# Layer 1's attention: every second tile squared by ACT straight out of PSUM, with reordered transposes, sends and sums in layer 0

## The chip, the cores and the metric

The kernel runs on one core of one Trainium2 chip. The metric is the device time of one execution in microseconds, as the median of several runs. PE is the matrix engine (TensorE), DVE the vector engine, ACT the scalar engine, POOL is GpSimd and SP issues transfers. L12 is line 12 of the kernel before.

## The reference

A decoder of two layers works on x, 32 sequences of 100 tokens with 256 values each. A layer is three residual steps, each on a layer norm of x:

```python
x = x + _L0_attn_ref(_layernorm(x), w_qkv, w_proj)              # causal, 16 heads of 16
x = x + _L0_xattn_ref(ctx_768, _layernorm(x), mask, ...)        # over 361 context rows
x = x + _L0_ffn_ref(_layernorm(x), ...)                         # attention, then 8 experts
x = x + _L1_attn_ref(_layernorm(x), ...)
x = x + _L1_xattn_ref(_layernorm(x), ctx_768, ...)
x = x + _L1_ffn_ref(_layernorm(x), ...)                         # 8 experts with hidden layer
```

`_L0_ffn_ref` contains a second causal attention of 16 heads (with rotary queries and keys), a layer norm, a gate that picks the best 2 of 8 experts for every token, and another layer norm:

```python
x1 = _layer_norm(x + attn_out, ln1_w, ln1_b)
_, top_idx = jax.lax.top_k(softmax(x1 @ gate_w.T + gate_b), 2)
moe_out = sum(gate * (x1 @ expert_w + expert_b) for the two)
return _layer_norm(x1 + moe_out, ln2_w, ln2_b)
```

Layer 1's attention sends every head's queries and keys through a small network and a rotation, and uses sums of squares:

```python
def prep(t):
    h1 = jnp.tanh(jnp.einsum('bshd,do->bsho', t, w1) + b1)
    return jnp.einsum('bsho,on->bshn', h1, w2) + b2
qq = jnp.sum(qe ** 2, -1); kk = jnp.sum(ke ** 2, -1)    # qe, ke: prep(Q), prep(K), rotated
attn = jax.nn.softmax(s / s, axis=2)                    # s = qq * kk
```

## The kernel before

The 32 sequences (B) stand in 8 groups (NG) of 4 (G); a group's tile has GT = 400 columns, four sequences of 100 tokens. The stages follow one another: layer 0's attention to about 285 us, its cross attention to 740, the attention in its ffn to 1040 with a last iteration to 1055, the blocks of the experts to 1176, layer 1's attention to 1528, its cross attention to 2700, and its ffn. Each engine runs its instructions in the order in which the program names them, except for POOL and SP, whose issues the helper `in_order` also keeps in that order. A wait of one instruction so holds everything behind it on its engine.

**`heads_attention`** serves layer 0's attention and the ffn's. One iteration handles one sequence s (`i = s % 4` is its place in the group) as a software pipeline. PE computes the scores of s + 1 (`scores`), DVE adds the mask (`masked`, L372), then takes the negated maximum of each row (L383), and POOL adds it (L384, both in `lowered`). ACT takes exponentials (`exponentials`, L389), in two halves of 8 heads. For s itself `turn_weights` transposes the exponentials on PE in four rows r of four heads each (L396; rows 0 and 1 read the first half, 2 and 3 the second), and ACT copies each row out of PSUM to eT (L401). `sums` multiplies them by the values (L412) and ACT copies the result to back (L417). For s - 1, `divided` transposes back (L425), DVE takes a reciprocal (L430) and multiplies (L432) to o; `turn_sums` transposes o (L438, copy L444) and `output` projects it (L230). All of these PSUM tiles come from one rotating set, `mm_tile`, so that a transpose can begin only when the tile's former content has been read. `fill(s, part)` is called at four places of an iteration and puts in work of other stages.

In the ffn, `fill` follows a table, `plan`, whose keys are the distance of groups and whose entries are (i, part). `res` adds the attention's output to xl (L1396), whose norm `ahead_norm` and `rows_of` turn (L776 transposes xl). `gating` picks experts and places, and **`send0(g, i, behind, which)`** writes the rows of sequence i of group g to their experts' places in memory, with one indirect DMA of POOL for each of the two choices k (L1517), each behind a small memset (L1513). Groups 0 to 4 fill the first list, 5 to 7 the second.

**The expert blocks** are 65 (ALL), of 128 rows of one expert; the first list has M = MOST[0] = 39 of them. Block n fetches its rows six or more blocks ahead, `turned0` transposes them (L1620) and DVE (even n, L1628) or ACT (odd n, L1626) evicts the transposes with 1 added, `product` multiplies by the expert's weights (L230), ACT copies y out (L1646) and issues its DMA. After each block a hand-written table, `todo`, calls further work: the remaining `gating`, and from M + 5 on the sums of groups 0 and 1 (`weighed`, L1296), their second norm (`second_norm`, `second_scaled` on ACT, L199, and `second_added`), and `project_group(0, 0..10)`, which prepares group 0 for layer 1's attention: its norm xn (L190), the transposes of xn (part 2, L1191), the queries and keys (qk, L1205), the mean rows xm (L1211), vm and own (L1231). `halves` places the sends of the last groups and the fetches of the sums (`outputs_back`, L1287), paced by a copy of one value of the next block's tile.

**Layer 1's attention** has 16 turns for each group. A turn calls `second` for the tile of four turns before, then `first`: eight score products (L1928) and two tanh on ACT (L1934). `second` adds products (L1947) into one PSUM tile in two calls; with the second (o = 1, turns 1, 3, 5, ...) DVE evicts the tile with bias b2h to y (L1960), and squares it (L1971) into one quarter of sq. The last group's last tile does both on ACT (L1958, L1969); groups 6 and 7 rotate y before they square it. A tile is named by m (0 to 3) and r2 (0, 1). `head_sums` adds a group's squares on PE and DVE copies the sums out (L2008). `around` places the next group's `project_group` parts and the last group's sums between the turns.

Of the kernel before, what the change touches and what calls it, by code (L numbers as in the profile page):

```python
# [14 lines left out]
AF = mybir.ActivationFunctionType  # L15
ALU = mybir.AluOpType
# [3 lines left out]
B, T, D = 32, 100, 256  # L20
S2, DC = 361, 192
G = 4
NG = B // G
GT = G * T
# [42 lines left out]
def kernel(ctx: ExitStack, tc: tile.TileContext, io: dict, out: bass.AP):  # L67
# [218 lines left out]
    def heads_attention(pool, w, wo, bias, norm, turn, res, fill, ready=0, order=()):  # L286
# [102 lines left out]
            nc.scalar.activation(ex, sms.pop((s, hf)), AF.Exp, scale=0.25)  # L389
            exs[s, hf] = ex  # L390

        def turn_weights(s):
            for r in range(4):
                pt = mm_tile()
                for j in range(4):
                    nc.tensor.transpose(  # L396
                        pt[:T, j * T : (j + 1) * T], exs[s, r // 2][:, 4 * (r % 2) + j, :],
                        ident[:T, :T],
                    )
                eT = pool.tile([T, 4, T], F32, tag="eT", name="eT", bufs=5)  # L400
                nc.scalar.copy(eT.rearrange("p j q -> p (j q)"), pt[:T, :GT])  # L401
                eTs[s, r] = eT
            exs.pop((s, 0)), exs.pop((s, 1))

        def sums(s):

# [48 lines left out]
        with in_order(*order):  # L455
            for part in range(4 if ready < 1 else 0):
                norm(0, part)
            turned_[0] = turn(0)
            for m in range(4):
                queries_or_keys(0, m)  # L460
            if ready == 2:
                norm(1, 3)
            values(0)
            ps = scores(0)
            for hf in range(2):
                masked(0, hf, ps[hf])
                lowered(0, hf)
                exponentials(0, hf)
            if ready == 2:
                turned_[1] = turn(1)  # L470
                for m in range(2):
                    queries_or_keys(1, m)
            for part in range(4 if ready < 2 else 0):
                norm(1, part)
            for s in range(B + 1):
                g, i = s // G + 1, s % G
                more = s + 1 < B
                if more:
                    ps = scores(s + 1)
                    masked(s + 1, 0, ps[0])  # L480
                if g < NG and (bias is None or g == 1):
                    if i == 0 and g not in turned_:
                        turned_[g] = turn(g)
                    for m in (((2,), (3,), (), ()) if ready == 2 else ((0,), (1,), (2, 3), ()))[i]:
                        queries_or_keys(g, m)
                if i >= 1 and bias is None and g + 1 < NG:
                    norm(g + 1, i - 1)
                fill(s, 0)
                if 1 <= s <= B:
                    divided(s - 1)  # L490
                if more:
                    lowered(s + 1, 0)
                    masked(s + 1, 1, ps[1])
                if s < B:
                    turn_weights(s)
                fill(s, 1)
                if more:
                    lowered(s + 1, 1)
                    values(s + 1)
                if 1 <= s <= B:  # L500
                    turn_sums(s - 1)
                if more:
                    exponentials(s + 1, 0)
                if s < B:
                    sums(s)
                fill(s, 2)
                if 1 <= s <= B:
                    output(s - 1)
                if more:
                    exponentials(s + 1, 1)  # L510
                if i == 3 and bias is None and g + 1 < NG:
                    norm(g + 1, 3)
                    turned_[g + 1] = turn(g + 1)
                fill(s, 3)
# [788 lines left out]
        )  # L1303

    def second_scaled(g, half_):
        scaled(x1back[g], x1back[g], range(2 * half_, 2 * half_ + 2), last_sums[g])

    def second_added(g, half_):
# [6 lines left out]
    with tc.tile_pool(name="f0x", bufs=1) as fixed, tc.tile_pool(name="f0", bufs=2) as pool:  # L1315
# [298 lines left out]
        def turned0(n):  # L1614
            if n >= ALL:
                return
            xg = xgs.pop(n)
            pt = mm_tile()
            for c in range(2):
                nc.tensor.transpose(  # L1620
                    pt[:, c * P : (c + 1) * P], xg[:, c * P : (c + 1) * P], ident
                )
            xT = tiles.tile([P, 2, P], F32, tag="xgT", name="xgT", bufs=4)
            flat = xT.rearrange("p c t -> p (c t)")
            if n % 2:
                nc.scalar.activation(flat, pt[:, : 2 * P], AF.Identity, bias=ones8[:, 0:1])  # L1626
            else:
                nc.vector.tensor_scalar_add(flat, pt[:, : 2 * P], 1.0)  # L1628
            xgTs[n] = xT
# [25 lines left out]
        def ahead_norm(g, part):  # L1655
# [15 lines left out]
            },  # L1671
            0: {(3, 2): ((rows_of, 0),)},
            -3: {
                (0, 2): ((send0, 0),), (1, 2): ((send0, 1),), (2, 2): ((send0, 2),),
                (3, 2): ((send0, 3),),
            },
            -1: {
                (1, 2): ((rows_of, 1),), (1, 3): ((rows_of, 2),), (2, 2): ((rows_of, 3),),
# [9 lines left out]
        def fill(s, part):  # L1688
# [4 lines left out]
            for away, events in plan.items():  # L1693
                g = w + away
                if 0 <= g < NG and (away < 1 or g >= 2):
                    for f, *args in events.get((i, part), ()):
                        if s < B or f is not gating:
                            f(g, *(args if s < B or f is not send0 else (1,)))
            if s < 2 and part == 2:
                output_bias(s)  # L1700
            if s == B and part == 0:
                send0(SPLIT[1], 0)
            if (s, part) in CONSTANTS:
                make_constants(CONSTANTS[s, part])
            if s < 2 * E and s % 2 == 0 and part in (1, 2):
# [27 lines left out]
        with tc.tile_pool(name="f0t", bufs=2, side="right") as tiles, in_order(pool_, sp_):  # L1733
# [17 lines left out]
                M + 10: ((second_norm, 0, 1),), M + 11: ((second_scaled, 0, 0),),  # L1751
                M + 12: ((second_scaled, 0, 1), (second_added, 0, 0)),
                M + 13: ((second_added, 0, 1),), M + 14: ((project_group, 0, 0),),
                M + 15: ((weighed, 1, 0), (project_group, 0, 1)),
                M + 16: ((project_group, 0, 2),),
                M + 17: ((project_group, 0, 3), (weighed, 1, 1)),
                M + 18: ((project_group, 0, 4),),
                M + 19: ((project_group, 0, 5), (second_norm, 1, 0)),
                M + 20: ((project_group, 0, 6), (weighed, 1, 2)),
                M + 21: ((project_group, 0, 7),),  # L1760
                M + 22: ((weighed, 1, 3), (project_group, 0, 8)),
                M + 23: ((project_group, 0, 9), (second_norm, 1, 1)),
                M + 24: ((project_group, 0, 10), (second_scaled, 1, 0)),
                M + 25: ((second_scaled, 1, 1), (second_added, 1, 0), (second_added, 1, 1)),
            }
            halves = {}
            for when, group, first in (
                ((0, 1, 3, 4), g - 2, 2), ((8, 9, 11, 12, 14, 15, 17, 18), g - 1, 0),
                ((19, 21, 22, 24, 25, 27, 28, 30), g, 0),
            ):  # L1770
                for j, n in enumerate(when):
# [138 lines left out]
    with tc.tile_pool(name="a1", bufs=2) as pool:  # L1910
# [26 lines left out]
        def second(g, m, i):  # L1937
# [15 lines left out]
                return  # L1953
            if r2 == 0 and m % 2 == 0:
                sqs[g, m // 2] = pool.tile([P, 4, GT], F32, tag="sq", name="sq")
            y = pool.tile([P, GT], F32, tag="y", name="y")
            if n_last(g, m):
                nc.scalar.activation(y, pos_.pop((g, m, r2))[:, :GT], AF.Identity, bias=b2h)  # L1958
# [1014 lines left out]
```

## Time and profile before

| | us |
|---|---|
| median of 3 runs | 3266.95 |
| lowest, highest | 3263.18, 3269.54 |
| profiled execution | 3296.56 |
| its span, first to last instruction | 3294.8 |
| PE busy in the span | 3163.5 (96%) |
| DVE, ACT, POOL busy | 1812.7, 1641.7, 1335.3 |
| mean granted clock of PE | 0.984 |

All times of single instructions come from the profiled execution, which took 29.6 us longer than the median of the runs. The granted clock is the share of PE's full speed that the chip's throttle allowed. In the profile's lines, out<-in names the tile written and the tiles read, xN the number of instructions in the group, and the bracket the time for which the engine was idle before it and what ended that.

### The profile page before, as it was taken

Reading aid. Unit: us, or ns where it says so; the run is one execution under the profiler, and the core shown is the slowest. Engines: PE = TensorE matmul, PEld = TensorE weight load, DVE = VectorE, ACT = ScalarE, POOL = GpSimd, SP = SyncE. Lnnn points to the kernel's source line nnn. Section 1 sums busy time; section 2 is a strip of 40 time slices with the busy share of each in tenths; the row PEclk is TensorE's granted clock in tenths of the full one; section 3 lists DMA queues with packets and bytes.
Section 4 is the critical chain, followed back from the end, with each engine's and each line's share of the span. In section 5 each row is a group of like instructions: output and inputs, shape, how many; then the busy total and the mean of one; then the engine's idle time right before and its main releaser. Section 6 shows DMA issues by size and latency. Waiting matters only on the chain. (4 is left out here: it accounts for less than half of the span.)

```text
span 3294.8 us, 66334 instructions
## 1 busy us (share of the span) xinstructions
PE 3163.5 (96%) x25158; PEld 2158.5 (66%) x25158; DVE 1812.7 (55%) x5224; ACT 1641.7 (50%) x3705; POOL 1335.3 (41%) x1190
## 2 busy tenths in 40 slices
PE   8998999989998799999999999999999989999998
PEld 6775666656776543334666666666666658899998
DVE  6776666757886478876455555464645451011111
ACT  5665666666674456665545545454545432211111
POOL 3445888876775432201323333333333332012222
PEclk9999999999998989999999999999999999999999
DMA  9401212101012722100100100010000003456665
GB/s 301 159 15 53 53 51 56 48 2 59 25 34 64 223 79 53 30 2 15 36 17 20 34 15 25 15 30 23 18 25 21 25 22 103 134 182 188 179 189 152
DMA packets 165700, 228.71 MB, mean 69 GB/s; under 512 B 22846, under 2 KB 139618, under 8 KB 164998
## 3 DMA queue, kind: packets, MB, share of 16 engines
q1 hardware_dynamic: 133592, 185.22, 18.0%
q0 software_dynamic: 20304, 27.99, 4.0%
q10 hardware_dynamic: 11486, 11.23, 1.0%
q8 instruction: 204, 3.34, 0.4%
q14 instruction: 114, 0.93, 0.1%
HBM read 150.92 MB, written 73.41 MB: 68 GB/s over the span
## 5 line engine op out<-in xcount | busy, mean ns | idle before, releaser
L2345 POOL TENSOR_TENSOR ex<-ex,rc 100x1444 f32<-100x1444 f32 x128 | 332.3, 2596 | 697.8 <-DVE rc L2344 456.2
L2336 ACT ACTIVATE ex<-s,nmx 100x361 f32<-100x361 f32 x512 | 305.7, 598 | 116.4 <-DVE nmx L2327 115.4
L384 POOL TENSOR_TENSOR s<-s,nmx 100x800 f32<-100x800 f32 x128 | 199.9, 1563 | 204.5 <-DVE nmx L383 110.7
L1934 ACT ACTIVATE h<-sc,cols 128x800 f32<-128x800 f32 x256 | 222.6, 924 | 96.1 <-PE sc L1928 93.7
L2804 POOL DMA_INDIRECT out_x<-y,xg x53 | 82.8, 1562 | 425.7 <-DVE y L2803 232.4
L2327 DVE CUSTOM_DVE_ANT_0 s<-sc,mb 100x361 f32<-100x361 f32 x512 | 250.7, 528 | 7.6 <-PE sc L2320 7.6
L2786 ACT ACTIVATE hgT<-sc 128x1024 f32<-128x1024 f32 x53 | 54.3, 1025 | 326.5 <-PE sc L230 326.5
L2803 DVE TENSOR_SCALAR y<-mm,gx 128x256 f32<-128x256 f32 x53 | 25.7, 484 | 323.2 <-PE mm L230 323.2
L230 PE MATMUL sc<-xgT,w1b 128*128 128x128 f32 x1696 | 198.1, 275 | 0.4 <-DVE xgT L2771 0.4
L2320 PE MATMUL sc<-kT,qT 64*100 64x361 f32 x1024 | 197.6, 463 | 0.0
L230 PEld LDWEIGHTS sc<-xgT,w1b 128*128 128x128 f32 x1696 | 193.6, 192 | 0.7 <-DVE xgT L2771 0.6
L230 PE MATMUL mm<-wx,hgT 128*128 x848 | 191.6, 379 | 0.0
L2292 PE MATMUL mm<-x_wa,cT 128*128 128x512 f32 (+1 forms) x512 | 191.2, 496 | 0.0
L2308 DVE COPY vb<-mm 128x512 f32<-128x512 f32 x64 | 44.3, 692 | 251.7 <-PE mm L2297 251.7
L2352 PEld LDWEIGHTS mm<-ident,ex 100*128 100x128 f32 (+1 forms) x1536 | 144.9, 152 | 52.9 <-issue 30.2
L181 POOL TENSOR_TENSOR rs<-va,neghalf 100x4 f32<-100x4 f32 (+1 forms) x95 | 92.6, 977 | 206.9 <-DVE va L177 74.0
L1872 PE MATMUL mm<-cT,x_wa 128*128 128x361 f32 x512 | 176.3, 467 | 0.0
L2352 PE MATMUL mm<-ident,ex 100*128 100x100 f32 (+1 forms) x1536 | 169.2, 260 | 5.8 <-POOL ex L2345 5.2
L230 PEld LDWEIGHTS mm<-wx,hgT 128*128 128x128 f32 x848 | 157.2, 190 | 19.2
L2370 PEld LDWEIGHTS mm<-eT,vb 128*64 128x64 f32 (+1 forms) x3072 | 135.4, 137 | 33.6 <-issue 33.6
L2370 PE MATMUL mm<-eT,vb 128*64 128x100 f32 (+1 forms) x3072 | 148.0, 252 | 0.0
L2307 ACT COPY vb<-mm 128x512 f32<-128x512 f32 x64 | 37.5, 587 | 220.4 <-PE mm L2297 220.4
(429 smaller groups left out, 7325.6 us busy)
## 6 DMA issues: line engine op xcount, KB each, us to landing
w1b<-in_f_w SPq DMA_DIRECT2D x55, 1024.0 KB
rows_dram<-zero SPq DMA_DIRECT2D x32, 896.0 KB
cT<-in_ctxT SPq DMA_DIRECT2D x64, 180.5 KB
cT<-in_ctxT SPq DMA_DIRECT2D x128, 90.2 KB
xg<-rows_dram SPq DMA_DIRECT2D x65, 128.0 KB
y_dram<-y ACTq DMA_DIRECT2D x65, 128.0 KB
wx<-in_f_w SPq DMA_DIRECT2D x8, 1024.0 KB
xg<-sorted_dram SPq DMA_DIRECT2D x57, 132.5 KB
```

The costliest lines, as they stand in the source:

```text
L181: nc.gpsimd.tensor_tensor(rs[:np_, :n], va[:np_, :n], neghalf[:np_, :n], ALU.pow)
L230: nc.tensor.matmul(ps, lhsT[k], rhs[k], start=(k == 0), stop=(k == n - 1))
L384: nc.gpsimd.tensor_tensor(sm, sm, bc(nmx, 2, T), ALU.add)
L1872: nc.tensor.matmul(kTs[u][c][:, :S2], x1_wa[:, m * P : (m + 1) * P], cT[:, 0, :], start=True, stop=False,)
L1934: nc.scalar.activation(h1, both[r2][:, :, :GT], AF.Tanh, bias=col("a1_b1", o))
L2292: nc.tensor.matmul(ps[e][:kn, :n], cT[:, 0, at], x1_wa[:, 1024 + c0 : 1024 + c0 + n], start=True, stop=False,)
L2320: nc.tensor.matmul(ps[:T, e, :S2], qT[p0 : p0 + 64, m, tok], kT[p0 : p0 + 64, c, :], start=True, stop=True,)
L2327: nc.vector.tensor_tensor_reduce(s[:, e, :], ps[:T, e, :S2], mb, 1.0, 3.4e38, ALU.add, ALU.min, nmx[:, e : e + 1],)
L2336: nc.scalar.activation(ex[:, 2 * c + e, :], s[:, e, :], AF.Exp, bias=nmx[:, e : e + 1], scale=-1.0, accum_out=sm[:, 2 * c + e : 2 * c + e ...
L2345: nc.gpsimd.tensor_tensor(ex, ex, bc(rc, 2, S2), ALU.mult)
L2352: nc.tensor.transpose(pt[:kn, j * T : (j + 1) * T], ex[:, j, k0 : k0 + kn], ident[:T, :T])
L2370: nc.tensor.matmul(po[64 * e : 64 * e + 64, m * T : (m + 1) * T], vb[k][:kn, v0 + 64 * h : v0 + 64 * h + 64] if k < 2 else vb[2 + u % 2][: ...
```

## The change

The diff has six parts. In `heads_attention`, rows 0 and 1 of `turn_weights(s)` come before `divided(s - 1)`, and rows 2 and 3 stay where all four were (A). `second_scaled` of groups 0 and 1 runs on DVE, one instruction for each sequence with both factors from the norm's sums, in place of ACT (B). `turned0` evicts on ACT in all blocks over M + 2 = 41 (C). `send0` in `plan` is called eight times for a group with one choice each, in place of four times with two; the last iteration sends nothing, and the sends of group 5 that stood there and in blocks 0, 1, 3 and 4 stand in blocks 0 to 7 (D). `todo` has another order in blocks M + 15 to M + 25 (E). In layer 1's attention, in groups 0 to 5, ACT squares the tiles with r2 = 1 straight out of PSUM with the bias b2h, 24 in all; there is no y of them (F).

```diff
-        def turn_weights(s):
-            for r in range(4):
+        def turn_weights(s, rows=range(4)):
+            for r in rows:
...
-            exs.pop((s, 0)), exs.pop((s, 1))
+            if 3 in rows:
+                exs.pop((s, 0)), exs.pop((s, 1))
...
                 fill(s, 0)
+                if s < B:
+                    turn_weights(s, range(2))
                 if 1 <= s <= B:
                     divided(s - 1)
                 if more:
                     lowered(s + 1, 0)
                     masked(s + 1, 1, ps[1])
                 if s < B:
-                    turn_weights(s)
+                    turn_weights(s, range(2, 4))
...
     def second_scaled(g, half_):
+        if g < 2:
+            sh, rs = last_sums[g]
+            for i in range(2 * half_, 2 * half_ + 2):
+                xi = x1back[g][:, i, :]
+                nc.vector.tensor_scalar(
+                    xi, xi, rs[:T, i : i + 1], sh[:T, i : i + 1], ALU.mult, ALU.add
+                )
+            return
...
-            if n % 2:
+            if n % 2 or n > MOST[0] + 2:
                 nc.scalar.activation(flat, pt[:, : 2 * P], AF.Identity, bias=ones8[:, 0:1])
...
             -3: {
-                (0, 2): ((send0, 0),), (1, 2): ((send0, 1),), (2, 2): ((send0, 2),),
-                (3, 2): ((send0, 3),),
+                (0, 2): ((send0, 0, None, (0,)),), (1, 1): ((send0, 0, None, (1,)),),
+                (1, 2): ((send0, 1, None, (0,)),), (2, 1): ((send0, 1, None, (1,)),),
+                (2, 2): ((send0, 2, None, (0,)),), (3, 1): ((send0, 2, None, (1,)),),
+                (3, 2): ((send0, 3, None, (0,)),), (3, 3): ((send0, 3, None, (1,)),),
             },
...
-                        if s < B or f is not gating:
-                            f(g, *(args if s < B or f is not send0 else (1,)))
+                        if s < B or f not in (gating, send0):
+                            f(g, *args)
...
-            if s == B and part == 0:
-                send0(SPLIT[1], 0)
...
-                M + 15: ((weighed, 1, 0), (project_group, 0, 1)),
-                M + 16: ((project_group, 0, 2),),
-                M + 17: ((project_group, 0, 3), (weighed, 1, 1)),
-                M + 18: ((project_group, 0, 4),),
-                M + 19: ((project_group, 0, 5), (second_norm, 1, 0)),
-                M + 20: ((project_group, 0, 6), (weighed, 1, 2)),
-                M + 21: ((project_group, 0, 7),),
-                M + 22: ((weighed, 1, 3), (project_group, 0, 8)),
-                M + 23: ((project_group, 0, 9), (second_norm, 1, 1)),
-                M + 24: ((project_group, 0, 10), (second_scaled, 1, 0)),
-                M + 25: ((second_scaled, 1, 1), (second_added, 1, 0), (second_added, 1, 1)),
+                M + 15: ((project_group, 0, 1),), M + 16: ((weighed, 1, 0),),
+                M + 17: ((weighed, 1, 1),), M + 18: ((second_norm, 1, 0),),
+                M + 19: ((project_group, 0, 2),),
+                M + 20: ((project_group, 0, 3), (weighed, 1, 2)),
+                M + 21: ((project_group, 0, 4), (project_group, 0, 5)),
+                M + 22: ((weighed, 1, 3), (project_group, 0, 6)),
+                M + 23: ((project_group, 0, 7), (second_norm, 1, 1)),
+                M + 24: ((project_group, 0, 8), (second_scaled, 1, 0)),
+                M + 25: (
+                    (project_group, 0, 9), (project_group, 0, 10), (second_scaled, 1, 1),
+                    (second_added, 1, 0), (second_added, 1, 1),
+                ),
...
-                ((0, 1, 3, 4), g - 2, 2), ((8, 9, 11, 12, 14, 15, 17, 18), g - 1, 0),
+                (range(8), g - 2, 0), ((8, 9, 11, 12, 14, 15, 17, 18), g - 1, 0),
...
+            if g < NG - 2 and r2 == 1:
+                nc.scalar.activation(
+                    sqs[g, m // 2][:, 2 * (m % 2) + r2, :], pos_.pop((g, m, r2))[:, :GT],
+                    AF.Square, bias=b2h,
+                )
+                return
```

## The prediction

> **What bounds the kernel now.** I read the page's busy line first, then the table of windows cut at the stages that the diff touches, then the waits of PE in those windows, and last the timeline at each wait. The page's first line:
>
> ```profile
> PE 3163.5 (96%) x25158; PEld 2158.5 (66%) x25158; DVE 1812.7 (55%) x5224; ACT 1641.7 (50%) x3705; POOL 1335.3 (41%) x1190
> ```
>
> PE is the bound; no other engine is near. An edit helps only where it closes a gap of PE or lifts its clock, and hurts only where it opens one. The windows (stretch, its length, then busy us of PE, PEld, DVE, ACT, POOL, then the granted clock, DMA share, GB/s), first layer 0's attention, its ffn's attention and layer 1's attention, then four throttle windows:
>
> ```profile
> 20.00:325.00 305.00, 281.21 (x3334) 202.50 (x3332) 220.77 (x444) 177.84 (x358) 130.99 (x151) 0.96 0.41 128
> 745.00:1035.00 290.00, 266.50 (x3324) 201.78 (x3322) 240.68 (x528) 197.83 (x405) 199.57 (x283) 0.99 0.12 36
> 1192.00:1431.00 239.00, 229.31 (x2035) 89.38 (x2034) 196.24 (x437) 168.09 (x206) 63.34 (x63) 1.00 0.15 39
> ...
> 1046.84:1050.25 3.41, 0.48 (x4) 0.40 (x4) 0.42 (x1) 1.02 (x3) 1.14 (x3) 1.00 0.48 141
> 1050.25:1067.32 17.07, 14.39 (x50) 10.66 (x49) 7.21 (x35) 3.35 (x10) 4.91 (x9) 0.50 0.35 103
> 1149.24:1152.65 3.41, 0.57 (x3) 0.17 (x1) 3.24 (x12) 0.88 (x3) 0.64 (x1) 1.00 0.77 229
> 1152.65:1159.48 6.83, 5.90 (x20) 4.63 (x21) 4.28 (x11) 0.85 (x2) 5.08 (x8) 0.50 0.45 134
> ```
>
> So 23.8, 23.5 and 9.7 us of PE idleness are all that the three attentions can give. The last four rows show the second resource: a stretch of 3.41 us in which PE works 0.48 or 0.57 us is followed by 17.07 or 6.83 us at clock 0.50, when the products f_wo take 1.92 us instead of 1.03.
>
> The waits of PE in the ffn's attention and layer 1's (total us, times, longest):
>
> ```profile
> PE mm L396 <- ACT eT L401: 8.2, 17, 1.7
> PE mm L396 <- DVE o L432: 5.3, 8, 1.0
> ...
> PE mm L1947 <- DVE sum L2008: 6.4, 5, 1.4
> PE mm L1947 <- DVE qk L1205: 2.6, 5, 0.7
> ```
>
> L396 is `turn_weights`' transpose. It waits for DVE's o because `divided`, queued ahead of it, holds a mm buffer; this the diff reorders. The sum copies of layer 1 (1.4 each) it does not touch.
>
> **A: rows 0 and 1 of `turn_weights` ahead of `divided`, both attentions.** No instruction is added. The timeline of the ffn's attention at a token with i = 3:
>
> ```profile
> 931.22 0.86 PE L396 MATMUL mm<-ident,ex 100*100 100x100 f32 x8 [0.83 <-DVE o L432]
> ```
>
> Two mm buffers are held there by the transposes of xl (L776), so row 1 waits 0.83 for o and row 3 another 0.30 for eT. With rows 0 and 1 first I take 0.65 of the 1.13, over 7 such tokens 4.5; 0.27 each over 7 tokens with i = 1, 1.9; and of the four gaps around the sends' tokens s = 16, 28, 29, 30 (1.36, 1.31, 2.15, 0.79: 5.6) a quarter, 1.5. Sum −8; range −14 (nearly all of 13.5) to 0.
>
> The price: `divided` starts two rows, 2 × 0.345 = 0.69, later, and behind it on DVE stand `lowered`'s maximum (0.98) and the mask, then POOL's subtraction (1.52), then ACT's exponential (0.87), which the next token's rows need. In the ffn's attention those exponentials end 0.65 to 2.3 before PE wants them, so 0.69 is covered. In layer 0's attention the tightest place is behind i = 2:
>
> ```profile
> 50.41 0.26 DVE L430 RECIPROCAL rc<-mm 100x16 f32<-100x16 f32 x1
> ...
> 55.64 0.87 ACT L389 ACTIVATE ex<-s 100x800 f32<-100x800 f32 x1 [0.67 <-POOL s L384]
> ```
>
> This ends at 56.51 and PE reaches row 2 at 56.69: slack 0.18, a new stall of 0.51, at five tokens 2.5. At other tokens PE gains a little, as `divided` no longer stands between the scores and their use; I take +2 (−2 to +6).
>
> **D: sends one at a time, and none in the last iteration.** Each send is a POOL memset and a DMA issue of 1.0 to 1.1, some 1.3 together. Spread singly they stand between the two subtractions of `lowered` and delay the second by about 1; at the tokens looked at the exponential then waits for ACT's own queue: nothing. The last iteration loses four issues of the six seen here:
>
> ```profile
> 1047.20 0.99 POOL L1517 DMA_INDIRECT rows_dram<-x,pos  x1 [0.21 <-issue]
> 1049.23 0.49 ACT L417 COPY back<-mm 128x400 f32<-128x400 f32 x1 [7.15 <-remote]
> ...
> 1049.77 0.68 PE L425 MATMUL mm<-ident,back 128*100 128x128 f32 x4 [3.33 <-ACT back L417]
> ```
>
> PE had written back's input by 1043.2, yet ACT starts only 1.04 after the last of the issues; the same happened to DVE at 902.6, 1011.3, 1020.6 and 1029.9, each at the end of such a burst. Without it PE gets its 3.33 back, and the half clock behind it, which cost about half of the PE work in 17 us less its idle time, may shrink: −4.5, range −9 to 0. The four sends move to blocks 0 to 7, now eight singles, each paced behind a block and 2.7 us apart; the list they fill is first fetched for block 39: 0 (±2).
>
> **B, C and E: the end of the expert blocks.** B gives 8 norms from ACT (0.59) to DVE (0.41); C gives 12 evictions from DVE (0.42) to ACT (0.474): both engines are about half busy there (29.4 and 17.9 of 55.5). E starts group 1's sums and norm earlier and moves the transposes of xn from M+16 to M+19. They aim at this:
>
> ```profile
> 1153.56 1.52 PE L1191 MATMUL mm<-ident,xn 100*128 100x100 f32 x4 [3.75 <-DVE xn L190]
> ```
>
> The stall of 3.75 makes the idle window 1149.24, and the half clock after it costs some 2.9 more. Smaller waits, 1.35 and 1.15 for xgT, 0.81, then 1.38 and 1.22 at layer 1's first score products, sum to 5.9, with a second half clock from 1179.96 to 1190.20. New cost: `project_group` 9 and 10 are both behind the last block, and 10 needs vm (DVE 0.35) and own (POOL 0.62): 1.1 to 1.5, and xm (0.98) ahead of them. I take 3 of the 3.75, 2.9, and 2.4 of the small ones, less 1.3: −7. Range −12 to −2.
>
> **F: 24 squares on ACT.** For groups 0 to 5 and r2 = 1, DVE's two steps
>
> ```profile
> 1312.95 0.63 DVE L1960 TENSOR_SCALAR y<-mm,b2h 128x400 f32<-128x400 f32 x1
> 1313.61 0.58 DVE L1971 TENSOR_TENSOR sq<-y 128x400 f32<-128x400 f32 x1
> ```
>
> become one activation out of PSUM with a bias of the same 128x400, whose nearest row is the last group's:
>
> ```profile
> L1958 ACT ACTIVATE y<-mm,b2h x2: 594/594/594, 1513.5 to 1515.3; 128x400 f32<-128x400 f32 x2
> ```
>
> ACT gains 0.5 to 0.59 each, DVE loses 1.21. Square already runs in this stage (L1969, 0.532), with no table load between 20.7 and 2719.8. ACT's two tanh take 1.75 a turn, PE's bare turn 1.69: ACT is nearly level in the turns with nothing else in them. The squares fall in turns 3, 7, 11 and 15 of 16, which last 1.96, 2.38, 2.13 and 4.86 in the median group. In the last three ACT idles 0.70, 1.25 and 1.43 before its tanh: free. In turn 3 the next second products wait for the tanh: +0.47 × 6 groups = +2.8. DVE's relief removes the 2.6 of qk waits and up to 0.2 elsewhere, −2.8. Net 0; range −6 to +6 (12 squares seen, or relief of twice as many turns).
>
> [...]
>
> **Sum**, against the profiled execution of 3296.56 (span 3294.8): +2 − 8 − 4.5 − 7 + 0 = −17.5. That execution is 0.9% above the median of 3266.95; the same saving on the median gives 3249.4, rounded to 3249. Its own range is 3236 to 3260.
>
> **The rivals.**
>
> *The end of the blocks gives nothing.* If `project_group` 10 behind the last block or group 1's earlier sums (waiting for their rows) open an idle window of their own, the −7 becomes +2: −8.5, 3258. For it: DVE is 3.24 of 3.41 busy in window 1149.24. Against: the transposes move three blocks, 6 to 8 us, back, and their input was 3.75 late.
>
> *ACT becomes layer 1's bound.* If every square delays the next tanh: 24 × 0.47 = +11.3 and no relief: −6.2, 3261. For it: 1.75 against 1.69 in bare turns. Against: three of four turns idle on ACT.
>
> *Slower: `divided` late.* The chain `divided`, maximum, subtraction, exponential becomes the path in both attentions once its slack is under 0.69. It is 0.18 at five tokens and at least 0.65 in the ffn's; if half of the 62 tokens pay it in full, 31 × 0.69 = +21.4 in place of the −6 of A. With −4.5 and −7: +10, 3277.
>
> That the change does not do what it says: the squares' condition (g < 6, r2 = 1) and the new places are plain in the code, so I give this nothing.
>
> **How the numbers follow.** Forecast 0.58, first rival 0.14, second 0.13, third 0.15. A measurement here can tell 0.2%, 6.5 us: faster is under 3260.4, slower over 3273.5. Faster: 0.58 and 0.10 of the first rival, less what the forecast's edges lose to the second's gain, 0.68; same 0.17; slower 0.15. The range of all cases is 3232 (the forecast's parts near their better ends) to 3272.
>
> **What would show it.** Right: the waits of L396 for o fall from 5.3 to under 2 in 745:1035; no idle of 3.33 ahead of the last L425, and less than 17 us of half clock behind it; the stall on xn under 1; layer 1's groups still 42.4 us apart. Wrong: L396 waiting for eT or L389's exponentials in layer 0's attention by more than 10; L1947 or L1928 waiting for h in layer 1's turns 3, 7, 11, 15; PE idle ahead of the last `project_group`.

## The result: 0.24% slower than the kernel timed beside it

The changed kernel takes 3276.49 us (median of 16 runs, 3268.60 to 3282.78), the kernel before, timed beside it, 3269.03 (16 runs): a ratio of 1.0024, 95% interval 1.0016 to 1.0031, where the forecast was 3249. The later runs came to five chips, and these fall into two kinds by the time of the same kernel before: 3268.6 to 3270.8 on three, 3288.6 and 3290.5 on two. I call them the quick and the late kind. The record names no chip for the first pair; its 3269.03 is of the quick kind. On a late chip the same change is faster: 0.9985 (0.9976 to 0.9994). Each chip was met once, so whether the kind belongs to the chip, to the core used on it or to the time of the runs is not settled; "late chip" is a name for the two groups of times.

The profile after, first the page's busy line, then the table of windows with the same three stretches, the idle window ahead of the blocks and the half clock behind it (rows as in the prediction's table: stretch, length, busy us of PE, PEld, DVE, ACT, POOL, granted clock, DMA share, GB/s):

```profile
PE 3160.9 (96%) x25158; PEld 2164.3 (66%) x25158; DVE 1796.9 (55%) x5172; ACT 1650.8 (50%) x3733; POOL 1334.8 (41%) x1190
```

```profile
20.00:325.00 305.00, 282.43 (x3322) 203.73 (x3324) 225.18 (x458) 176.67 (x362) 135.57 (x153) 0.96 0.41 129
745.00:1035.00 290.00, 262.09 (x3290) 200.74 (x3288) 253.54 (x543) 199.46 (x407) 199.40 (x289) 0.98 0.10 29
1192.00:1431.00 239.00, 235.97 (x2088) 92.46 (x2086) 172.19 (x398) 183.37 (x233) 65.23 (x65) 1.00 0.15 39
1031.50:1034.91 3.41, 0.68 (x7) 0.43 (x5) 3.17 (x18) 2.80 (x6) 2.57 (x6) 1.00 0.17 43
1034.91:1058.81 23.90, 20.98 (x106) 16.03 (x107) 11.55 (x46) 5.73 (x14) 9.38 (x20) 0.50 0.40 117
```

In the fixed window 745 to 1035 PE is less busy than before (262.1 against 266.5), but the window cuts the two kernels at different places: from the first scores of the ffn's attention to its last it is 256.6 busy in 278.0 us, and was 257.1 in 279.1. The half clock around the last iteration is 23.9 us long. PE's waits in 745 to 1035 follow. Line numbers are those of the kernel profiled, in which the edits shift lines: L426, L433, L1407 and L1443 here are L425, L432, L1396 and L1432 of before.

```profile
PE mm L426 <- DVE xl L1407: 4.1, 5, 1.2
PE mm L396 <- DVE o L433: 3.1, 6, 0.6
...
PE mm L396 <- ACT x1T L1443: 1.5, 4, 0.6
```

The wait for o fell from 5.3 to 3.1, not to under 2, which was the prediction's sign of being right; and a part of the fall is the chip, as a profile of before on a quick chip (e9, below) has 4.1. A wait of `divided`'s transposes for xl (up to 1.2 each) is new: 2.6 in all comes with A alone (e10, e13), 4.1 with D. The span, 3278.5, is shorter than the first profile's 3294.8 while the timed kernel is slower, so these two profiles can't be subtracted; the first question was why.

### The profile page after: what moved, and what is told of

It is laid out like the page before. It is cut to its first block, busy times and chain, and to the rows that moved or that the text cites. A ratio compares the mean times of both kernels' runs of the same rounds, so it can differ in the third digit from the quotient of the medians.

```text
span 3278.5 us, 66386 instructions
## 1 busy us (share of the span) xinstructions
PE 3160.9 (96%) x25158; PEld 2164.3 (66%) x25158; DVE 1796.9 (55%) x5172; ACT 1650.8 (50%) x3733; POOL 1334.8 (41%) x1190
## 5 line engine op out<-in xcount | busy, mean ns | idle before, releaser
L2354 ACT ACTIVATE ex<-s,nmx 100x361 f32<-100x361 f32 x512 | 305.8, 598 | 115.9 <-DVE nmx L2345 115.9
L389 ACT ACTIVATE ex<-s 100x800 f32<-100x800 f32 x128 | 111.6, 872 | 92.3 <-POOL s L384 88.8
L2325 ACT COPY vb<-mm 128x512 f32<-128x512 f32 x64 | 37.5, 586 | 220.4 <-PE mm L2315 220.4
```

The lines of the kernel that those rows point to most:

```text
L2354: nc.scalar.activation(ex[:, 2 * c + e, :], s[:, e, :], AF.Exp, bias=nmx[:, e : e + 1], scale=-1.0, accum_out=sm[:, 2 * c + e : 2 * c + e ...
```

## Experiments on the difference between the chips

**The kernel before as a control** (no edit), three times, and **the whole change again**.

> The kernel before, unchanged, as a control: its time against itself, and a second profile. Theory 1 (the change's loss lies where the first profile of before does not show it, because that profiled execution, 29.6 us over the median, is not typical): ratio 1.000 within 0.001, and a profile whose span is near 3268, shorter than the 3294.8 of the first in some stages; the stages of the changed kernel, which looked 0 to 5 us shorter than the first profile's, are then no shorter or longer than this one's. Theory 2 (the profile of before is typical of profiled executions, and the gains of 3.7 in layer 0's attention, 4 in the blocks and 5 in layer 1's attention are real, but a cost outside of what the profile sees turns them round): span 3290 to 3298 again, each stage within 1 us of the first profile.

Measured, late chip: 1.0002 (0.9992 to 1.0011), 3291.1 against 3288.6, span 3283.3. So the time of before differs by chip, and one profile of it from another by some 10 us.

> The whole change again, beside the kernel before. The first four runs were on a chip on which before takes 3288.6, and there A alone and A to E gained 8 (0.9976, 0.9972) and F nothing, so the parts do not add up to the loss of 7.5 that was measured where before takes 3269.0. Theory 'chip' (the parts add; the sign depends on the chip): where before is near 3289 the whole change is faster by 6 to 9, ratio 0.997 to 0.998; where it is near 3269 it is slower by 7, ratio 1.0024. Theory 'together' (F with A to E costs what neither costs alone, for instance because the blocks' new order and the squares put work on ACT at one place): ratio 1.002 wherever it runs.

Measured, a second late chip: 0.9985 (0.9976 to 0.9994), 3284.7 against 3290.5. The sign is that of "chip"; the gain, 5, is below its 6 to 9.

> The kernel before once more, mainly for a profile on this chip. Theory 'gate phase' (the 3.41 us windows of the clock gate run free, and an execution differs from the next by where they fall): the stretches at half clock lie at other places than in the first two profiles, whose sum between 740 and 1500 was 58 and 55 us, and iterations with none of them in it agree within 0.1 us. On a chip where before takes 3269 the stages that are 20 us shorter show here.

Measured, the same late chip: 0.9998 (0.9988 to 1.0008). In the first profile all 17 half-clock stretches start on one grid, from 12.60 to 3289.40 us in 960 steps of 3.4133. The remainder of these starts by the step is 2.36 there, 1.85 in e1, 1.40 here and 0.68 in the changed kernel's; within one profile all have the same remainder.

> The kernel before, for its profile on this chip. On the two chips tried, where before takes 3289 and 3290.5, its DVE copies of layer 1's sums (L2008) start 2 us after PE is done in five groups, and in the ffn's last iteration ACT and DVE idle 7 and 5 us although PE was done; in the changed kernel's first profile, from where before takes 3269, no copy is late. Theory 'late copies' (that is the difference between the chips): if before takes 3269 here, its groups of layer 1 are 41.2 in place of 42.4 and the ffn's last iteration has no idle of 3.3 ahead of L425; if it takes 3289, both are as before.

Measured: a quick chip, 3269.8 against 3268.8, 1.0003 (0.9993 to 1.0013). Its profile answers the question. The timeline of layer 1's turn 15 in e6 (late chip) and then in e9 (quick chip), same kernel:

```profile
1251.49 0.89 PE L2002 MATMUL mm<-sq,a_sum 128*32 128x100 f32 x32
1252.56 1.01 POOL L1287 DMA_INDIRECT yb<-y_dram,from  x1 [0.30 <-issue]
1254.49 0.26 DVE L2008 COPY sum<-mm 128x100 f32<-128x100 f32 x1 [2.50 <-PE mm L230]
1254.81 0.88 PE L1947 MATMUL mm<-h,w2h 128*32 128x400 f32 x8 [1.36 <-DVE sum L2008]
```

```profile
1239.72 0.89 PE L2002 MATMUL mm<-sq,a_sum 128*32 128x100 f32 x32
1240.69 0.26 DVE L2008 COPY sum<-mm 128x100 f32<-128x100 f32 x1 [0.46 <-PE mm L2002]
1240.79 1.01 POOL L1287 DMA_INDIRECT yb<-y_dram,from  x1 [0.30 <-issue]
```

The rows are PE's sums of squares, POOL's last issue, DVE's copy of the sums and, on the late chip, the products that wait for it. PE's sums end at 1252.38 and 1240.61. The copy starts 2.1 us later on the late chip, 0.9 after the last of four indirect DMA issues, and 0.08 us later on the quick one, although the issues stand at the same place. The same is seen in the last iteration of the ffn's attention, e6 then e9:

```profile
1036.30 1.56 PE L412 MATMUL mm<-eT,va 100*32 100x100 f32 x32
1043.47 0.49 ACT L417 COPY back<-mm 128x400 f32<-128x400 f32 x1 [6.74 <-remote]
```

```profile
1031.47 1.56 PE L412 MATMUL mm<-eT,va 100*32 100x100 f32 x32
1033.10 0.49 ACT L417 COPY back<-mm 128x400 f32<-128x400 f32 x1 [1.20 <-PE mm L412]
```

ACT starts 5.6 after PE's end on the one, 0.07 on the other, with sends running in both. Between the profiles e6 and e9 the ffn's attention from its first to its last scores is 276.8 and 272.5, the last iteration (to the first product of a block) 31.6 and 26.1, layer 1's turns 331.6 and 325.1: 16 of the 18 us between them. Of these 16, 9.0 are waits of PE for the starts that the rows show late: 6.1 for five copies of the sums and 2.9 for back; the rest was not traced start by start. The first profile of before has waits for late copies of 6.4 us in all and idles marked "remote" of 7.15 and 4.96, so it is of the late kind, and the first timed pair is of the quick kind. The phase of the half clock is not what parts these two: its remainder is 1.40 in e6 and 1.39 in e9. What holds the starts back stays open.

**The issues out of the way**, on the kernel before:

```diff
-        0: ((rows_back,), (outputs_back, 0), (outputs_back, 1)),
-        1: ((outputs_back, 2), (outputs_back, 3)), 2: ...
+        0: ((rows_back,),), 2: ...
...
+            if n == 0:
+                for i in range(4):
+                    outputs_back(2, i)
+            if at == 9 and g + 3 < NG:
+                for i in range(4):
+                    outputs_back(g + 3, i)
```

> The kernel before with one edit: in layer 1 the four outputs_back of a group (eight indirect DMAs of POOL) are called at turn 9 of the group before, in place of turns 0 and 1 after it, so that they no longer run while the sums' copy L2008 waits. Theory 'burst' (the copy is late because these issues run then): the 1.4 stalls of L1947 go, five of them, turn 15 is 3.6 in place of 4.8, ratio 0.998 where before takes 3289; 1.000 where it takes 3269. Rival (the lateness has another cause, or moves to whatever waits in turns 10 to 13): turn 15 unchanged or another turn longer by as much, ratio 1.000.

Measured on a quick chip: 0.9995 (0.9984 to 1.0005), as "burst" has it there; a late chip, where it would decide, was not met again.

## Experiments on the parts

**A alone**, twice:

```diff
                 fill(s, 0)
+                if s < B:
+                    turn_weights(s, range(2))
                 if 1 <= s <= B:
                     divided(s - 1)
...
-                    turn_weights(s)
+                    turn_weights(s, range(2, 4))
```

> Part A alone: rows 0 and 1 of the transposes ahead of divided, in both attentions. Theory 'late divided' (my third rival): slower by 5 to 12 us, ratio 1.0015 to 1.0035, with iterations of the ffn's attention at i = 2 longer by 1.7 each, as the changed kernel's profile has them. Theory 'rows first helps' (my forecast): faster by about 6, ratio 0.998. If the loss is from the clock gate: more half-clock stretches of 3.41 us between 745 and 1035 than the one of the first profile.

Measured, late chip: 0.9976 (0.9965 to 0.9986).

> Part A alone again. Gate theory: near 0.9976 as on the first chip, since layer 0's attention is 3.7 shorter in every profile with A, and nothing in that stage sends rows. Theory 'chip': where before takes 3269 the ffn's attention gives back 5 to 10 with A (its tokens with i = 2 longer, with half-clock windows in them): ratio 1.0005 to 1.002.

Measured, quick chip: 0.9987 (0.9978 to 0.9996). A gains on both; my third rival falls. Layer 0's attention, from its first scores to its last, is 248.3 in e9 and 244.6 here; it is 248.3 in all eight profiles without A and 244.4 to 244.8 in all twelve with it. PE's waits from 24 to 264, e9 and then e10:

```profile
PE mm L396 <- DVE qT L323: 3.2, 13, 0.4
```

```profile
PE mm L396 <- ACT ex L389: 2.7, 6, 0.4
```

The stall on the exponentials that I had costed came, at 2.7; but 13 waits of the transposes for DVE's eviction of qT, 3.2 in all, went with the reordering, and I had not counted them. That balances the stall and does not make up the 3.6: between the first and the last scores PE is busy 232.8 of 248.3 us in e9 and 230.4 of 244.6 in e10, so idle time gives 1.2 of it. The other 2.4 are in the busy time of the same instructions, and why that is shorter stays open.

**F alone, and A to E without F**:

```diff
+            if g < NG - 2 and r2 == 1:
+                nc.scalar.activation(
+                    sqs[g, m // 2][:, 2 * (m % 2) + r2, :], pos_.pop((g, m, r2))[:, :GT],
+                    AF.Square, bias=b2h,
+                )
+                return
```

> Part F alone: ACT's 24 squares in layer 1's attention on the kernel before. Theory 'squares' (the loss comes from layer 1, where ACT is level with PE): slower by 7 to 11 us (ratio 1.002 to 1.0035), and layer 1's groups 0 to 5 longer than in a profile of before of the same kind. Theory 'relief' (as the profile of the changed kernel shows, groups of 41.6 in place of 42.4): faster by 3 to 5 us, ratio 0.9985 to 0.999. My forecast was 0.

Measured, late chip: 1.0004 (0.9995 to 1.0013). Neither theory; the forecast's 0 lies in the interval.

> Parts A to E without F. Theory 'squares': the loss of 7.5 is gone, ratio 0.998 to 1.0005. Theory 'relief': the loss lies in layer 0 and is larger without F: slower by 10 to 13 us, ratio 1.003 to 1.004.

Measured, late chip: 0.9972 (0.9962 to 0.9983), below what either theory had.

> A to E without F again. By the groups of layer 1 (turn 4 of every group is 0.42 longer with F, in all profiles with it, nothing else is shorter) F costs 2.5 on every chip: so this is 2.5 faster than the whole change: 0.9975 where before takes 3289, 1.0016 where it takes 3269.

Measured, quick chip: 1.0014 (1.0005 to 1.0023). So on a quick chip the loss stands without F, and since A gains there, it is in D or in B, C and E: 10 us between e10 (3264.5) and e11 (3274.2).

**D alone; B, C and E alone**, both on a late chip:

> Part D alone: sends one at a time, none in the last iteration. My forecast: faster by 4.5 (0 to 9), ratio 0.9986, from the boundary. Rival: the half clock after the last iteration comes all the same and takes the gain, ratio 0.9995 to 1.0005; in that case the profile has at least 20 us at half clock between the last scores and the block products, as the whole change's has 23.9.

Measured: 1.0005 (0.9996 to 1.0014), the rival's time but not its sign: behind the last scores the half clock lasts 17 us at most, not 20. The last iteration is 28.2 in place of 31.6, the attention 280.3 in place of 276.8. That the sends gave the gain back there is not shown by this one profile: e2 and e8, whose code for the ffn's attention is that of before, have 285.9 and 279.8 on late chips.

> Parts B, C and E alone: the end of the blocks. My forecast: faster by 7 (2 to 12), ratio 0.9979. Rival 'moved stall': the wait for xn goes, but the last two project_group parts behind the last block put an idle window there, as in the whole change's profile with 13.7 us at half clock from 1168: ratio 0.9995 to 1.001.

Measured: 0.9995 (0.9984 to 1.0006), as the rival has it.

**The halves of D, and the blocks, each on top of A**, on a quick chip (before 3270.8):

```diff
             -3: {
-                (0, 2): ((send0, 0),), (1, 2): ((send0, 1),), ...
+                (0, 2): ((send0, 0, None, (0,)),), (1, 1): ((send0, 0, None, (1,)),),
+                (1, 2): ((send0, 1, None, (0,)),), (2, 1): ((send0, 1, None, (1,)),), ...
```

> A and of D only the table: sends of a group one at a time in parts 1, 2 and 3; the last iteration keeps its four. Theory 'single sends' (the one in part 1 stands between the two halves of lowered on POOL, the second subtraction and DVE's work beside it end later, xl is late and the transposes of back wait 1.2 in place of 0.7 at i = 2, and the half clock follows): 4 to 6 slower than A alone where before takes 3269, 1.0000 to 1.0006; where it takes 3289, 0.998 to 0.999. Rival 'last sends': as A alone, 0.9987 and 0.9976.

Measured: 1.0022 (1.0010 to 1.0035), the theory of single sends, and more than the 1.0000 to 1.0006 that it gave.

```diff
-                        if s < B or f is not gating:
-                            f(g, *(args if s < B or f is not send0 else (1,)))
+                        if s < B or f not in (gating, send0):
+                            f(g, *args)
...
-            if s == B and part == 0:
-                send0(SPLIT[1], 0)
...
-                ((0, 1, 3, 4), g - 2, 2), ...
+                (range(8), g - 2, 0), ...
```

> A and of D only the rest: pairs as before in the table, no sends in the last iteration, eight singles in blocks 0 to 7. Theory 'single sends': as A alone or up to 2 faster, 0.998 to 0.9987 where before takes 3269; where it takes 3289 the late copy of the last iteration is gone and 3 more gained, 0.9965 to 0.9976. Rival 'last sends': 4 to 8 slower than A where before takes 3269, through blocks 0 to 16.

Measured: 0.9995 (0.9982 to 1.0008).

```diff
-            if n % 2:
+            if n % 2 or n > MOST[0] + 2:
...
-                M + 16: ((project_group, 0, 2),),
+                M + 19: ((project_group, 0, 2),),
```

(with the rest of B and E as in the change)

> A with B, C and E. Theory 'moved stall': as A alone, within 2 us: 0.9983 to 0.9992 where before takes 3269, 0.997 to 0.998 where it takes 3289. My forecast of minus 7 for the blocks would be 0.9966 and 0.9955. If the blocks' order is what costs on the first chip: 1.001.

Measured: 0.9992 (0.9980 to 1.0003).

> A with the early outputs_back of e12, the version that the runs point to. If the two add: where before takes 3269, 0.9987 and 0.9995 give 0.998 (3262.5); where it takes 3289, A's 0.9976 and the five stalls of 1.2 at the sums' copy, 6, give 0.996.

Measured: 0.9997 (0.9983 to 1.0011); here the runs of before spread from 3260 to 3282. e13, e15 and e16 all hold A and none of them is clear of 1, so that A gains on a quick chip rests on e10. The single sends stand out: e14 is 6.8 to 8.9 us over these three.

Where they cost it is seen between e13 and e14, whose ffn's attention differs in nothing else and has 271.2 and 274.8 us. The other profiles agree: on quick chips and with A the stage lasts 270.2 to 273.3 in the six with pairs and 274.8 to 278.1 in the three with single sends. PE's waits from 880 to 1016, e13 then e14:

```profile
PE mm L426 <- DVE xl L1399: 2.0, 3, 0.7
PE mm L396 <- DVE o L433: 1.7, 3, 0.6
```

```profile
PE mm L426 <- DVE xl L1399: 3.6, 3, 1.2
PE mm L396 <- ACT x1T L1435: 1.6, 4, 0.6
PE mm L396 <- DVE o L433: 1.4, 3, 0.6
```

The timeline at the token with i = 2 shows why xl is late. In e13:

```profile
972.86 3.75 POOL L384 TENSOR_TENSOR s<-s,nmx 100x800 f32<-100x800 f32 x2
974.24 0.98 DVE L804 TENSOR_TENSOR xrT<-xrT,xwT 128x800 f32<-128x800 f32 x1
975.15 2.54 DVE L1404 TENSOR_TENSOR xl<-xl,out_row 100x1024 f32<-100x1024 f32 x1
977.61 0.41 DVE L1399 TENSOR_TENSOR xl<-xl,mm 100x256 f32<-100x256 f32 x1
978.07 0.64 PE L426 MATMUL mm<-ident,back 128*100 128x128 f32 x4 [0.67 <-DVE xl L1399]
```

and in e14, with one send moved ahead of the two subtractions:

```profile
970.68 1.03 POOL L1520 DMA_INDIRECT rows_dram<-x,pos  x1 [0.19 <-issue]
971.74 3.00 POOL L384 TENSOR_TENSOR s<-s,nmx 100x800 f32<-100x800 f32 x2
972.80 2.80 DVE L804 TENSOR_TENSOR xrT<-xrT,xwT 128x800 f32<-128x800 f32 x1
975.52 1.21 DVE L1404 TENSOR_TENSOR xl<-xl,out_row 100x1024 f32<-100x1024 f32 x1
976.66 0.41 DVE L1399 TENSOR_TENSOR xl<-xl,mm 100x256 f32<-100x256 f32 x1
977.12 0.64 PE L426 MATMUL mm<-ident,back 128*100 128x128 f32 x4 [1.19 <-DVE xl L1399]
```

The scores of the token start at 975.61 and 974.14. By that mark POOL's pair starts 2.75 and 2.40 ahead, DVE's L804 at 1.37 and 1.34. In e13 L804 starts as the first subtraction ends (974.24 against 974.37), takes 0.98, and the second subtraction stretches: the pair takes 3.75 in place of 3.00. In e14 L804 starts in the middle of the first and ends 0.86 after the second: 2.80. L1404 is shorter in return, but xl is ready 2.92 after the mark in place of 2.41. Other tokens are longer too, s = 17, 25, 28 and 29 by 0.82, 0.38, 0.77 and 0.73, with waits for x1T and back that are new or longer; s = 16 is 0.44 shorter.

On the late chips the single sends cost nothing that shows: with A the stage lasts 275.9 in e4 with pairs, 275.6 and 275.7 in e3 and e5 with singles. The tokens with i = 2 are longer there as well (s = 22 and 26 take 10.8 in e3 and 9.9 in e4), but the last three tokens take 24.3 in place of 26.2. So the loss belongs to the quick kind.

**The change with pairs again**, on a quick chip (before 3268.6), the edit of e14 undone in the whole change, and then without F too:

> The whole change but with the sends in the table in pairs in part 2, as before (the last iteration still sends nothing, and blocks 0 to 7 have the eight singles). Single sends as the cause: where before takes 3269 to 3271, the loss of the whole change goes: its 1.0024 less the 0.0022 to 0.003 that e14 shows over A, 0.9990 to 1.0005. Where before takes 3289 it is 0.9965 to 0.998, as the other parts gain there. If the parts of the change together have a cost of their own: still 1.0015 or more.

Measured: 0.9998 (0.9989 to 1.0007), against 1.0024 (1.0016 to 1.0031) of the whole change.

> The same without F: another 2.5 us less (0.42 in turn 4 of groups 0 to 5), ratio 0.9983 to 0.9995 where before takes 3269 to 3271, 0.996 to 0.997 where it takes 3289; groups of layer 1 41.15 in place of 41.57, or 42.3 in place of 42.7.

Measured: 0.9993 (0.9984 to 1.0002), groups of 41.14 in place of 41.56, but a median only 0.35 us lower than in e17, not 2.5. The loss went with the single sends. None of these is measurably faster than before on a quick chip but A alone, 0.9987; on the late chips A to E without F, 0.9972, and A alone, 0.9976, are the quickest measured.

## Why the prediction was wrong, by its steps

Between the forecast of −17.5 and the measured +7.5 lie 25 us. In the timed runs on quick chips the single sends are 7 to 9 of them, B, C and E 5 to 7, the last iteration about 5, A less than 2, and F from next to nothing (0.35) to 2.5.

**D, "nothing" in the ffn's attention: the step that failed.** I held the delay of the second subtraction against the exponential alone and found it covered. The send also moves both subtractions against DVE's queue, and xl and x1T behind it were not covered. Measured, on quick chips: 3.6 us between two profiles, 7 to 9 in the timed runs. Part of the difference can be the half clock: at i = 2 the changed kernel's profile has, in the table of windows,

```profile
901.80:905.21 3.41, 2.23 (x46) 1.91 (x46) 3.41 (x4) 3.41 (x8) 2.48 (x5) 1.00 0.05 11
905.21:908.62 3.41, 3.41 (x14) 2.76 (x15) 3.14 (x5) 1.81 (x5) 0.67 (x1) 0.50 0.06 19
942.75:946.17 3.42, 3.28 (x14) 2.93 (x15) 3.10 (x6) 2.05 (x5) 0.39 (x1) 0.50 0.11 30
980.30:983.72 3.42, 3.20 (x14) 2.85 (x15) 3.10 (x6) 0.98 (x2) 0.30 (x1) 0.50 0.11 30
```

three stretches 37.5 us apart, which is 11 steps of 3.413 and nearly what four iterations last there (37.8 and 37.6), so one bad phase repeats in every group: 11.9 to 12.0 for the tokens 18, 22 and 26, where e14 has 10.8. e11 has them too; e3, e5 and e14 have single sends and none at these tokens. e14's profiled execution, 3272.6, is 3.8 under the median of its runs, so it is one of the better ones. How often the stretches come in the timed runs was not seen, and the rest of the 7 to 9 is not settled.

**D, −4.5 at the last iteration.** Near on a late chip for the iteration itself (31.6 to 28.2 in e7, where PE no longer waits for back), though e7 as a whole gained nothing; wrong on a quick one, where there is no late start to remove: with A it lasts 27.0 with the sends (e10, e13) and 27.2, 27.2 and 28.6 without (e17, e18, e15), and 30.2 in the whole change with its long half clock. In the timed runs e15 takes 0.3 more than e13. The trace I read was of a chip on which these starts are late; that they depend on the chip, no row of one profile could show. I treated them as a property of the kernel.

**A.** Layer 0's attention: predicted +2, measured −3.6, for a reason that the waits show in part only. The ffn's attention: predicted −8; in profiles on quick chips 272.5 before (e9, e12) and 270.2 to 273.3 in the six with A and pairs, so −2 to +1. The sum, −6, is near the measured −4.4 on a quick chip and −8 on a late one, for the wrong reasons, so that its nearness is luck: what A gained at i = 3 (0.16 a token in place of 0.65) and, from s = 9 on, at i = 1 (0.16 to 0.53) it gave back at i = 2 (0.1 to 0.5 each) and at i = 0 from s = 16 on (1.05 there, then 0.13 to 0.26). The slack of 0.65 that I took to cover 0.69 in the ffn's attention was also 0.04 short of it.

**B, C and E, −7.** Measured 0 within the noise (0.9995 in e8; e16 is 1.8 and 2.1 us under e13 and e15): the blocks to layer 1's first turn last 116.0 in e9 and 115.7 in e16, and in the other profiles on quick chips 113.5 to 120.0 without these parts and 115.9 to 121.0 with them. PE's waits from 1095 to 1170, e9 then e16:

```profile
PE mm L1191 <- DVE xn L190: 3.8, 1, 3.8
PE mm L230 <- DVE xgT L1628: 3.2, 4, 1.2
PE mm L1620 <- DMA xg<-rows_dram: 1.8, 5, 0.7
PE mm L230 <- ACT xgT L1626: 1.6, 2, 1.1
PE sc L1928 <- ACT y L1646: 1.4, 1, 1.4
PE sc L1928 <- ACT h L1934: 1.2, 1, 1.2
```

```profile
PE mm L230 <- ACT xgT L1637: 4.2, 3, 2.6
PE mm L1631 <- DMA xg<-rows_dram: 2.0, 2, 1.9
PE mm L1194 <- DVE xn L190: 1.8, 1, 1.8
PE mm L230 <- DVE xm L1214: 1.2, 1, 1.2
PE mm L230 <- POOL own L1234: 1.1, 1, 1.1
```

The wait for xn was halved (I took 3 of 3.75, it gave 2.0), and the 2.6 ahead of layer 1's scores went. Against that the two waits behind the last block rose from 0.4 and 0.2 to 1.2 and 1.1, 1.7 more where I had put 1.3; the waits for xgT, 4.8 on two engines, are 4.2 on ACT alone, so C moved them and removed little. The waits listed for this window sum to 13.6 and 10.9; that the 2.7 between them is lost to the half clock fits its length, 6.8 and 10.2 us from 1134 on in e9 against 3.4, 3.4 and 13.7 from 1126 on in e16, but is not shown by itself. Of my rivals the first comes nearest: no gain here, with new waits behind the last block.

**F, 0.** Measured +2.5 in the rows: groups 1 to 5 with it are 41.56 to 41.57 in place of 41.15, and the whole of it is turn 4, 2.61 in place of 2.19. The timed runs do not resolve it: 1.0004 (0.9995 to 1.0013) alone, and 0.35 us between e17 and e18. The squares of the changed kernel:

```profile
L1969 ACT ACTIVATE sq<-mm,b2h x24: 593/593/599, 1186.1 to 1425.3; 128x400 f32<-128x400 f32 x24
```

The price of a square (0.593) and the one turn in four that pays (0.42 × 6 against my 0.47 × 6) were right; the relief of −2.8 did not come. PE's waits for qk in 1150 to 1500 are 3.1 us in six waits in e9 and 3.1 in six in the changed kernel: taking y and the square off DVE left them as they were, so they were not what made qk late.

## What to carry to other kernels

A DMA issued by POOL in the middle of a pipelined loop was not free here though its own delay was covered (e14 takes 6.8 to 8.9 us more than e13, e15 and e16): list what POOL does next, and which DVE instructions then fall under it instead of between (L804, 2.80 us in place of 0.98). Before a stall is costed from one profile, run the unchanged kernel on a second chip; a stall that is not there on the other one is worth nothing there. And an order found at one place, such as rows first, is best measured apart from what is joined to it: here it gained 4 to 8 us alone, and on the quick chips the sends took as much or more.

## What the runs showed of the hardware

- The same kernel took 3269 on some chips and 3290 on others, while the runs of one chip spread over 11 to 22 us. 16 of the 18 us between two profiles lie in stages where POOL issues indirect DMAs, 9 of them as PE's waits for DVE and ACT instructions that start late; the copy of the sums started 2.1 us after PE's end on a late chip and 0.08 on a quick one.
- DVE's L804 took 0.98 or 2.80, by where it began against POOL's subtractions: in e14 it began in the middle of the first and ended 0.86 after the second, and in e13 it began as the first ended, and the second subtraction stretched instead, to 2.14 from 1.52. Why the one stretches beside the other is not shown.
- The half-clock stretches of a profile start on a grid of 3.413 us whose offset is not the same in all profiles (2.36, 1.85, 1.40 and 0.68 above): all 17 of the first profile, and all 17 of the changed kernel's, there from 24.57 to 3270.64. A window, one step of this grid, that PE filled did not end the half clock: in the changed kernel's stretch of 23.9 us the window from 1038.32 has 3.42 us of PE work in 3.42, and the next is at 0.50 too:

```profile
1038.32:1041.74 3.42, 3.42 (x43) 2.89 (x42) 2.54 (x13) 1.62 (x4) 1.92 (x3) 0.50 0.33 92
1041.74:1045.15 3.41, 2.51 (x9) 1.57 (x8) 1.34 (x5) 0.54 (x1) 0.00 (x0) 0.50 0.26 77
```

- In the changed kernel the window from 901.80 had 2.23 us of PE work and was followed by half clock. A window of e5 at the same place of the program, also with 2.23, was not:

```profile
904.17:907.58 3.41, 2.23 (x46) 1.90 (x45) 3.41 (x4) 3.41 (x8) 2.16 (x5) 1.00 0.10 27
907.58:911.00 3.42, 3.33 (x19) 2.18 (x17) 3.35 (x6) 2.00 (x6) 1.31 (x1) 1.00 0.01 4
```

So the profile's share of PE work, 2.23 of 3.41 in both, does not decide it alone.
